# Copies that may run on either engine, norms behind the gathers on VectorE, and unread products in TensorE's pauses

## The chip, the cores and the metric

The kernel runs on one core of a Trainium2 chip. The core has engines that work side by side, each through its own instructions in order: TensorE (PE) multiplies matrices and transposes, VectorE (DVE) and ScalarE (ACT) work elementwise and reduce, GpSimd (POOL) does elementwise work too and issues the indirect DMAs, and SyncE (SP) issues the other DMAs. PE writes into PSUM, which here is eight banks of 128 x 512 f32; DVE and ACT can read them, POOL works on SBUF. Engines wait for each other on semaphores.

The metric is the time of one execution in device microseconds, as the median of several. The program is the same in every execution, and so is its order of instructions.

## The reference

`x` is (8, 128, 128) f32, eight blocks of 128 tokens with 128 features, and `ctx` is (8, 77, 128). There are four layers, each a cross-attention to the context and a second part, both added to `x`:

```python
x = x + L0_xattn(_layernorm(x), ctx)       # 16 heads of 8
x = x + L0_ffn(_layernorm(x))              # soft mixture: 512 slots, exact gelu
x = x + L1_xattn(_layernorm(x), ctx)       # 16 heads of 64, gated
x = x + L1_ffn(_layernorm(x))              # top 3 of 64 experts, capacity 64
x = x + L2_xattn(_layernorm(x), ctx)       # 16 heads of 8, rope, two norms, relu ffn
x = x + L2_ffn(_layernorm(x))              # 6 layers of local attention, 16 heads of 64, window 32
x = x + L3_xattn(_layernorm(x), ctx)       # 8 heads of 64
x = x + L3_ffn(_layernorm(x))              # 2 layers of local attention, 8 heads of 64, window 64
```

The parts that the change touches most are these two. The routed experts of layer 1 (cut):

```python
top_l, top_i = jax.lax.top_k(xf @ gate_w + gate_b, 3)
gates = softmax(top_l)
pos = (cumsum(oh, axis=0) * oh).sum(-1) - 1           # a token's place with its expert
buf = zeros((64, 64, 128)).at[fe, pos].set(xf[tok], mode='drop')
h = gelu(einsum('ecd,edh->ech', buf, w1) + b1)
y = einsum('ech,ehd->ecd', h, w2) + b2
out = zeros_like(xf).at[tok].add(y[fe, pos] * gates)  # three gathered rows a token
```

And one local layer of layer 2 or 3 (cut):

```python
h = shift_token(x)                  # the second half of the features comes from the token before
q, k, v = split(h @ Wqkv)
q, k = rotary(l2norm(q) * qs, l2norm(k) * ks)
x = x + softmax(masked(q k^T * 8)) v @ Wo      # windows: own and the one before
h = layernorm(shift_token(x)) @ W1 + b1
a, g = split(h)
x = x + (a * gelu(g)) @ W2 + b2
```

The cross-attention of layer 2 norms twice inside: `x = norm(query + o)`, a small relu network, `norm(x + ff)`.

## The kernel before

**A planner writes the order.** `Plan` holds steps. A step has a list of engines that may run it with an estimated duration in ns for each (`{"ACT": 591, "DVE": 682}`), the values that it reads and writes, and a function that emits its instructions. `arranged()` plays the steps through when the kernel is built: at each planned time it gives each free engine the earliest ready step it may run, and where a step may run on several engines, the first that is free takes it. A step that opens a value needs a room for it, which for PE's results is one of the eight PSUM banks (`"mm"`). `emit()` then emits the instructions in that order. On the chip each engine holds to its order whatever the real durations are. There are two such plans in the program that runs: "front" (layers 0 and 1 with routing and experts) and "later" (layers 2 and 3). A second, general form of the layers follows under a branch and is not executed for these inputs.

**What the helpers emit.** `Work.copy` brings a PSUM bank to SBUF: on ACT at L749 or, where the caller gave a DVE duration, on DVE at L751. `Work.turn` makes up to four transposes on PE (L762), `Work.mm` one matmul (L769). `Work.normed` and `Work.scaled` make a layer norm: statistics on DVE (L783, L785), then a step on POOL with four small instructions (L776 variance, L790 its power -1/2, L791 and L792 minus mean times that), then the scaling, on ACT (L800) with scale and bias, or on DVE (L802) with mean and scale; with `norms_on_act`, which the later plan sets, on ACT alone.

**Front.** Layer 0's cross-attention (`attend_8`: scores L855, exp L863, sums and products L871, DVE L876 to L878, and the watch on the sums, L881 and L882, on POOL), its soft mixture (up L1215, gelu L1219 with table loads, down L1229), layer 1's cross-attention (`attend_64`), then `Routed`: gate sums and choice on DVE (L1287 to L1348, with L1326 on PE), twelve indirect DMAs on POOL that scatter the rows to their experts (L1363), rows back in (L1421), transposes, and for each expert up (L1461), gelu (L1474) and down (L1482), with the weights streaming in by 256 KB (L1445).

**Later.** For each of eight blocks `one` gathers three rows a token from the expert results (`Routed.gathered`: L1512, an indirect DMA on POOL, and L1517 on DVE, which adds it with its gate), norms, turns, rotates (`Context.rotated`: two DVE products L1549 and an add on POOL, L1553), attends and projects; `layer` does two blocks' norms, relu network and the addition to `x` (L1622 to L1650, with the affine of the norms at L1650 and the addition at L1642 on POOL); `begin` starts local attention for them. In local attention (`Local`) `shifted` turns `y` and copies it with the shift by one token (two copies at L749), `projected` multiplies by Wqkv (L1847), `queries_keys` squares (L1868, ACT), rotates (L1869, L1871 on DVE, L1874 on POOL), scales by the inverse root (L1887, POOL), turns, and copies to `qT` (L749); then scores, exp and products by windows (L1952 to L2019), `divided` (L1981) and the projection (L1933). `gated` is the second part: L2051, gelu on ACT between two table loads (L2058, L2059), L2064, three DVE products L2066, down L2074. The order inside is by halves: four blocks of attention (`some(4)`), then `gated` for four. A half of one layer is called a half layer below.

The two copies in `shifted`, which run on ACT alone:

```python
self.copy(lambda: hs()[0:64], lambda: tp()[0:64], [tp], [hs], 180 + 103 * n)
self.copy(lambda: hs()[64:128, :, 1:P], lambda: tp()[64:128, :, 0 : P - 1], [tp], [hs], 180 + 103 * n)
```

The step in `scaled` that stands on POOL, with `under` being one tensor_scalar for a layer norm:

```python
under(nc, va()[:, 0:n], mv()[:, 0:n, 1])
nc.gpsimd.tensor_tensor(va()[:, n : 2 * n], va()[:, 0:n], c.mhalf[:, 0:n], ALU.pow)
nc.gpsimd.tensor_scalar(nb(), mv()[:, 0:n, 0], -1.0, None, ALU.mult)
nc.gpsimd.tensor_tensor(nb(), nb(), va()[:, n : 2 * n], ALU.mult)
```

## Time and profile before

| what | value |
|---|---|
| median of 3 runs | 1497.15 us (1496.13 to 1500.06) |
| profiled execution | 1488.41 us, of which the span is 1486.4 |
| mean granted TensorE clock in it | 0.977 |
| PE busy | 1389.6 us (93%) |
| DVE, ACT, POOL busy | 918.6, 918.3, 825.9 us |
| routing, first scatter to last | 259.66 to 274.75 us |
| first weights of the experts issued | 281.39 us |
| last result of the experts on its way | 371.55 us |
| gathers, first and last | 374.5 and 422.9 us |
| one half layer of layer 2's local attention, from 675.61 us | 64.98 us |

The profile is of one execution, taken by the hardware; its own time lies 8.74 us under the median of the three runs. The page gives each engine's busy time, then the span in 40 slices of 37.16 us with the busy share in tenths, and the TensorE clock that was granted in each slice. Groups of instructions carry the line of the kernel, the engine and the tiles; behind the bar stand the busy time, the mean duration and the idle time of the engine just before them. Windows cut the span into stretches.

### The profile page before, as it was taken

The numbers are of one execution on the slowest core, as the hardware profiler recorded it, in microseconds if no ns is written. First come the engines' busy times: TensorE is split into PE (matmuls) and PEld (weight loads), VectorE is DVE, ScalarE is ACT, GpSimd is POOL, SyncE is SP. The second block draws the span as 40 slices with busy tenths as digits, with TensorE's granted clock in tenths as the row PEclk, the third lists the DMA queues.
The fourth block names the chain that finished last, engine by engine and source line by source line (L and its number), as shares of the span: only waits on it lengthen the run. The fifth ranks groups of instructions, "written<-read, shape, count | busy, mean of one in ns | idle before, by whom it ended". The sixth has DMA issues, their size and how long they took to land.

```text
span 1486.4 us, 39191 instructions
## 1 busy us (share of the span) xinstructions
PE 1389.6 (93%) x15991; PEld 955.2 (64%) x15991; DVE 918.6 (62%) x1998; ACT 918.3 (62%) x1913; POOL 825.9 (56%) x1282
## 2 busy tenths in 40 slices
PE   8999997798889999999999999999999998889995
PEld 6776675565576666667566666756666666566654
DVE  7542676433459765685958668595866855658563
ACT  4665654343456675766667676666766675667663
POOL 5210235310788975765849586584948662628471
PEclk9999998799799999999999999999999999999997
DMA  9500001597501001000100100010000011000000
GB/s 321 175 1 1 9 5 54 184 337 263 190 13 72 2 2 58 17 2 2 58 17 2 45 31 2 2 58 16 2 2 23 11 65 40 23 2 2 1 9 11
DMA packets 44111, 79.07 MB, mean 53 GB/s; under 512 B 4582, under 2 KB 21542, under 8 KB 42768
## 3 DMA queue, kind: packets, MB, share of 16 engines
q1 hardware_dynamic: 38032, 71.21, 14.0%
q0 software_dynamic: 1536, 3.15, 0.7%
q8 instruction: 128, 2.10, 0.6%
q10 hardware_dynamic: 4352, 2.10, 0.5%
q14 instruction: 63, 0.52, 0.1%
HBM read 67.63 MB, written 8.81 MB: 51 GB/s over the span
## 4 chain that ended last, share of the span: by engine, by line
PE 39%; DVE 17%; POOL 12%; ACT 6%; issue 3%; DMA 2%; POOLq 0%; ACTq 0%; DVEq 0%; SPq 0%
PE mm L1847 7%; PE mm L762 6%; DVE big L1871 4%; DVE big L1869 4%; PE mm L1933 4%; DVE few L1873 4%; POOL big L1874 3%; PE mm L2074 3%; POOL big L1887 3%; PE mm L2019 3%; PE mm L1958 3%; PE mm L2051 3%; PE mm L2064 2%; POOL tiny L790 2%; DMA big<-in_experts_dram 1%
## 5 line engine op out<-in xcount | busy, mean ns | idle before, releaser
L749 ACT COPY big<-mm 128x512 f32<-128x512 f32 (+4 forms) x519 | 278.4, 561 | 220.9 <-PE mm L762 127.3
L1874 POOL TENSOR_TENSOR big<-big,big 128x512 f32<-128x512 f32 x224 | 284.2, 1276 | 225.5 <-DVE big L1871 218.1
L1847 PE MATMUL mm<-wide,big 128*128 128x512 f32 x672 | 317.0, 598 | 8.4 <-ACT big L749 8.4
L762 PE MATMUL mm<-ident,big 128*128 128x128 f32 (+1 forms) x1430 | 204.3, 279 | 26.8 <-DVE big L751 5.3
L1887 POOL TENSOR_TENSOR big<-big,few 128x512 f32<-128x512 f32 x224 | 227.2, 1043 | 1.6
L762 PEld LDWEIGHTS mm<-ident,big 128*128 128x128 f32 (+1 forms) x1430 | 161.4, 142 | 102.9 <-POOL big L1887 35.9
L1869 DVE TENSOR_TENSOR big<-mm,big 128x512 f32<-128x512 f32 x224 | 152.9, 683 | 56.7 <-ACT big L1868 56.2
L1847 PEld LDWEIGHTS mm<-wide,big 128*128 128x128 f32 x672 | 117.3, 191 | 103.6 <-issue 79.4
L1868 ACT ACTIVATE big<-mm 128x512 f32<-128x512 f32 x224 | 133.1, 597 | 77.3 <-PE mm L1847 70.3
L1871 DVE TENSOR_TENSOR big<-mm,big 128x512 f32<-128x512 f32 x224 | 152.7, 682 | 5.3 <-ACT big L1868 5.3
L1873 DVE TENSOR_REDUCE few<-big 128x8 f32<-128x512 f32 x224 | 151.4, 676 | 6.5 <-ACT big L1868 6.5
L1965 ACT ACTIVATE big<-mm 128x512 f32<-128x512 f32 x224 | 118.1, 610 | 28.0 <-PE mm L1958 27.4
L1933 PE MATMUL mm<-narrow,big 128*128 128x128 f32 x896 | 114.0, 279 | 3.7 <-DVE big L1981 3.7
L1933 PEld LDWEIGHTS mm<-narrow,big 128*128 128x128 f32 x896 | 105.6, 192 | 18.0 <-DVE big L1981 12.5
L1975 DVE TENSOR_TENSOR mm<-mm,big 128x512 f32<-128x512 f32 x64 | 44.6, 696 | 117.0 <-ACT big L1974 111.2
L2019 PEld LDWEIGHTS mm<-big,big 128*32 128x32 f32 x3072 | 85.9, 110 | 28.1 <-issue 27.4
L1958 PE MATMUL mm<-big,big 64*64 64x64 f32 (+2 forms) x3584 | 100.4, 238 | 1.1 <-ACT big L749 1.1
L1958 PEld LDWEIGHTS mm<-big,big 64*64 64x64 f32 x3584 | 94.2, 133 | 6.2 <-ACT big L749 2.0
L2019 PE MATMUL mm<-big,big 128*32 128x128 f32 x3072 | 92.8, 273 | 0.0
L1981 DVE SCALAR_TENSOR_TENSOR big<-mm,big 128x512 f32<-128x512 f32 x112 | 73.0, 687 | 5.6 <-PE mm L2019 0.6
L830 POOL TENSOR_TENSOR big<-big,tiny 128x308 f32<-128x308 f32 x40 | 28.5, 717 | 75.0 <-DVE tiny L827 34.2
L1471 DVE TENSOR_TENSOR big<-mm,p_col 128x512 f32<-128x512 f32 x32 | 20.7, 687 | 62.9 <-PE mm L762 53.0
(276 smaller groups left out, 2314.9 us busy)
## 6 DMA issues: line engine op xcount, KB each, us to landing
big<-in_experts_dram SPq DMA_DIRECT2D x128, 256.0 KB
wide<-in_l2a_dram SPq DMA_DIRECT2D x6, 1536.0 KB
narrow<-in_l2b_dram SPq DMA_DIRECT2D x6, 534.0 KB
narrow<-in_l2o_dram SPq DMA_DIRECT2D x6, 512.0 KB
kept<-big SPq DMA_DIRECT2D x16, 154.0 KB
big<-kept SPq DMA_DIRECT2D x16, 154.0 KB
p_w<-in_w_dram SPq DMA_DIRECT2D x1, 2048.0 KB
expert_rows<-big SPq DMA_DIRECT2D x8, 256.0 KB
```

The lines of the kernel that those rows point to most:

```text
L749: nc.scalar.copy(out(), in_())
L762: nc.tensor.transpose(tp()[:, k, :], v(k), c.ident)
L1847: self.plan.add({"PE": 860}, lambda e: nc.tensor.matmul(ps(), lhsT=hs()[:, j, :], rhs=wqkv()[:, o : o + 512], start=True, stop=True), [hs, ...
L1868: yield lambda e: nc.scalar.activation(sq(), heads(), AF.Square)
L1869: yield lambda e: nc.vector.tensor_tensor(t1(), heads(), spread(rot()[:, 2 * kind, :], 8, 1), ALU.mult)
L1871: yield lambda e: nc.vector.tensor_tensor(halves(t2()), halves(heads())[:, :, ::-1, :], sin(), ALU.mult)
L1873: yield lambda e: nc.vector.tensor_reduce(ss()[:, lo : lo + 8], sq(), AX.X, ALU.add)
L1874: yield lambda e: nc.gpsimd.tensor_tensor(t1(), t1(), t2(), ALU.add)
L1887: plan.add({"POOL": 1062}, lambda e, t=t, t1=t1, i=i: nc.gpsimd.tensor_tensor(t(), t1(), spread(r()[:, 8 * i : 8 * i + 8], 64, 2), ALU.mul ...
L1933: nc.tensor.matmul(out(), lhsT=oT()[:, k, :], rhs=wo()[:, 4 * g + k, :], start=(g == 0 and k == 0), stop=(4 * g + k == nch - 1))
L1958: nc.tensor.matmul(sc[s]()[at : at + 64, k, q:end], lhsT=kT()[lo : lo + 64, k, at : at + 64], rhs=qT()[lo : lo + 64, k, q:end], start=Fals ...
L2019: nc.tensor.matmul(avs[half]()[32 * t : 32 * t + 32, k, :], lhsT=vs[t // 2]()[:, at : at + 32], rhs=prs[t]()[:, k, :], start=True, stop=True)
```

## The change

The planner gets a sixth kind of decision. While the planned time lies before a limit (300 us in the plan "front", 60 us in "later", none in the general form), and PE has no step to pick for 400 ns after its last one, it places a matmul whose result nobody reads: `ones` times `ident`, 128 x 128, planned at 220 ns, into the PSUM bank that came free last. More of them follow at once until a step can be picked. In the order that results, 122 of them stand in the part that is executed: 14 ahead of PE's first real matmul, 29 more before some 160 us of the old trace (12 of them before the first L1229), 61 between the matmuls of routing and ahead of the first expert rows, and 18 in the later plan, where the gathers and layer 2's cross-attention are.

The norms behind the gathers (one of a block and two of two blocks for each pair of blocks, 16 in all) are scaled on DVE alone, with mean and scale, and their POOL step has no L791 and L792. The norms of `begin`, `gated` and of the front stay as they were.

The watch, and the add L1553, may run on POOL or DVE. The copies of `shifted` and the copies to `qT` may run on ACT or DVE. The planned duration of a gather goes from 1000 to 1290 ns.

In the order that results, instructions that are executed move like this: on DVE 44 more copies (L751), 17 more scalings (L802), 9 adds (L1553) and 4 pairs of watch instructions; on ACT 44 fewer copies and 17 fewer scalings; on POOL 16 fewer pairs of L791 and L792, 9 fewer adds and 4 fewer watch pairs. SP's list is the same. Of the copies of `shifted`, one pair of layer 2's `begin` and both pairs of layer 3's stand on DVE, the latter ahead of the three products L2066; of the copies to `qT` four and two in turn for each half layer. Where a step changes its engine or its planned time, others move in the order too.

```diff
     DRAIN = 100.0
+    IDLE, WARM = 400.0, 220.0
...
     def __init__(self, tc, rooms):
...
         self.latest, self.previous = {}, None
+        self.warm, self.until = None, 0.0
...
     def fixed(self, tile):
...
         first = 0
+        left, extra, done_on_pe = sum("PE" in s.ns for s in self.steps), 0, True
...
         def open_to(s):
...
                 if pick is None:
+                    if e == "PE" and t < self.until and t >= free[e] + (self.IDLE if done_on_pe else 0.0) and (
+                            rooms["mm"] and left and (coming or any(free[x] > t for x in free if x != e))):
+                        s = Step(first, {e: self.WARM}, self.warm(rooms["mm"][-1]), None, None, 0, None)
+                        s.start, s.engine, free[e], done_on_pe = t, e, t + self.WARM, False
+                        done.append(s)
+                        extra += 1
+                        heapq.heappush(times, free[e])
                     continue
+                if e == "PE":
+                    done_on_pe, left = True, left - 1
                 if e == "PE" and pick.mode not in (None, mode[e]):
...
                 heapq.heappush(times, free[e])
+                if e == "PE" and self.until:
+                    heapq.heappush(times, free[e] + self.IDLE)
                 done.append(s)
...
                         offer(g)
-        assert len(done) == len(self.steps), f"{len(done)} of {len(self.steps)} steps, rooms {rooms}"
+        assert len(done) == len(self.steps) + extra, f"{len(done)} of {len(self.steps)} steps, rooms {rooms}"
         return done
...
     def emit(self):
...
     KINDS = {"tiny": 8, "few": 32, "row": 128, "big": 512, "huge": 1232}
...
-    def __init__(self, c, pool, once, bufs, general):
+    def __init__(self, c, pool, once, bufs, general, warm_until):
         self.c, self.once, self.by_head, self.norms_on_act, self.general = c, once, (0, 1), False, general
         self.plan = Plan(c.tc, {"mm": 8, **bufs})
+        self.plan.until = 0.0 if general else 1e3 * warm_until
+        self.plan.warm = lambda slot: lambda e: c.nc.tensor.matmul(
+            self.buffers["mm"][slot][:, 0:P], lhsT=c.ones, rhs=c.ident, start=True, stop=True)
         self.buffers = {k: [pool.tile([P, n], F32, name=f"{k}{i}") for i in range(bufs[k])]
...
                       reads, writes, "full", opens)
...
-    def normed(self, outs, ins, reads, writes, a=1.0, b=EPS, n=4):
+    def normed(self, outs, ins, reads, writes, a=1.0, b=EPS, n=4, on_dve=False):
...
         self.scaled(outs, ins, reads, writes,
-                    lambda nc, t, v: nc.gpsimd.tensor_scalar(t, v, float(a), float(b), ALU.mult, ALU.add), n)
-
-    def scaled(self, outs, ins, reads, writes, under, n=4):
+                    lambda nc, t, v: nc.gpsimd.tensor_scalar(t, v, float(a), float(b), ALU.mult, ALU.add), n, on_dve)
+
+    def scaled(self, outs, ins, reads, writes, under, n=4, on_dve=False):
         c, nc, plan = self.c, self.c.nc, self.plan
...
             nc.gpsimd.tensor_tensor(va()[:, n : 2 * n], va()[:, 0:n], c.mhalf[:, 0:n], ALU.pow)
-            nc.gpsimd.tensor_scalar(nb(), mv()[:, 0:n, 0], -1.0, None, ALU.mult)
-            nc.gpsimd.tensor_tensor(nb(), nb(), va()[:, n : 2 * n], ALU.mult)
-
-        plan.add({"POOL": 930 + 150 * n}, root, [mv], [va, nb])
+            if not on_dve:
+                nc.gpsimd.tensor_scalar(nb(), mv()[:, 0:n, 0], -1.0, None, ALU.mult)
+                nc.gpsimd.tensor_tensor(nb(), nb(), va()[:, n : 2 * n], ALU.mult)
+
+        plan.add({"POOL": (500 if on_dve else 930) + 150 * n}, root, [mv], [va] if on_dve else [va, nb])
         for k in range(n):
...
                     nc.vector.tensor_scalar(outs(k), ins(k), mv()[:, k, 0:1], scale(k), ALU.subtract, ALU.mult)
...
-            plan.add({"ACT": 490} if self.norms_on_act else {"ACT": 490, "DVE": 450}, scaled,
-                     [*one, mv, va, nb], writes if len(writes) != n else [writes[k]])
+            plan.add({"DVE": 450} if on_dve else {"ACT": 490} if self.norms_on_act else {"ACT": 490, "DVE": 450}, scaled,
+                     [*one, mv, va] if on_dve else [*one, mv, va, nb], writes if len(writes) != n else [writes[k]])
...
     def softmax(self, sc, n, by_head=False):
...
         plan.add({"DVE": 282}, lambda e: nc.vector.tensor_tensor(oT(), av(), rs(), ALU.mult), [av, rs], [oT])
...
         def watch(e):
-            nc.gpsimd.tensor_tensor(cl(), cl(), rs(), ALU.add)
-            nc.gpsimd.tensor_tensor(c.total, c.total, cl(), ALU.add)
-
-        plan.add({"POOL": 650}, watch, [rs, self.total], [cl, self.total])
+            on = nc.gpsimd if e == "POOL" else nc.vector
+            on.tensor_tensor(cl(), cl(), rs(), ALU.add)
+            on.tensor_tensor(c.total, c.total, cl(), ALU.add)
+
+        plan.add({"POOL": 920, "DVE": 560}, watch, [rs, self.total], [cl, self.total])
         return self.projected_8(oT, wo, bias)
...
     def projected_8(self, oT, wo, bias):
...
                     in_offset=bass.IndirectOffsetOnAxis(ap=self.srci[:, b, k : k + 1], axis=0)).ins
...
-            plan.add({"POOL": 1000}, get, [w.landed], [g], tail=2300)
+            plan.add({"POOL": 1290}, get, [w.landed], [g], tail=2300)
             plan.add({"DVE": 382}, lambda e, k=k, g=g: nc.vector.scalar_tensor_tensor(
...
             t.append(tt)
-        plan.add({"POOL": 240 + 2.0 * n * m}, lambda e: nc.gpsimd.tensor_tensor(
+        plan.add({"POOL": 240 + 2.0 * n * m, "DVE": 145 + 1.1 * n * m}, lambda e: (nc.gpsimd if e == "POOL" else nc.vector).tensor_tensor(
             out() if m > 1 else out().unsqueeze(1), t[0](), t[1](), ALU.add), t, [out])
...
     def keys(self, h):
...
         x, (xh, xT, qT, y) = w.xs[b], (w.tile([P, P]) for _ in range(4))
         route.gathered(w, b)
-        w.normed(lambda k: xh(), lambda k: x(), [x], [xh], n=1)
+        w.normed(lambda k: xh(), lambda k: x(), [x], [xh], n=1, on_dve=True)
         tp = w.turn(lambda k: xh(), [xh], n=1)
...
         y1 = w.tile([P, n, P])
-        w.normed(lambda k, y1=y1: y1()[:, k, :], lambda k, y=y: y[k](), y, [y1], n=n)
+        w.normed(lambda k, y1=y1: y1()[:, k, :], lambda k, y=y: y[k](), y, [y1], n=n, on_dve=True)
         affine(w, y1, "L2_xattn_g1", "L2_xattn_b1", n)
...
         y3 = w.tile([P, n, P])
-        w.normed(lambda k, y3=y3: y3()[:, k, :], lambda k, y2=y2: y2()[:, k, :], [y2], [y3], n=n)
+        w.normed(lambda k, y3=y3: y3()[:, k, :], lambda k, y2=y2: y2()[:, k, :], [y2], [y3], n=n, on_dve=True)
         affine(w, y3, "L2_xattn_g2", "L2_xattn_b2", n)
...
         plan.add({"POOL": 150}, lambda e: nc.gpsimd.memset(hs()[64:128, :, 0:1], 0.0), [], [hs])
-        self.copy(lambda: hs()[0:64], lambda: tp()[0:64], [tp], [hs], 180 + 103 * n)
-        self.copy(lambda: hs()[64:128, :, 1:P], lambda: tp()[64:128, :, 0 : P - 1], [tp], [hs], 180 + 103 * n)
+        self.copy(lambda: hs()[0:64], lambda: tp()[0:64], [tp], [hs], 180 + 103 * n, 145 + 134 * n)
+        self.copy(lambda: hs()[64:128, :, 1:P], lambda: tp()[64:128, :, 0 : P - 1], [tp], [hs], 180 + 103 * n, 145 + 134 * n)
         return hs
...
     def projected(self, layer, hs, j, o, opens):
...
             qT = self.tile([P, 4, P])
-            self.copy(qT, tp, [tp], [qT])
+            self.copy(qT, tp, [tp], [qT], 591, 682)
             out.append(qT)
...
 @contextmanager
-def work(c, name, bufs, general=False):
+def work(c, name, bufs, general=False, warm_until=0.0):
     with c.banks("ps_" + name), c.tc.tile_pool(
...
     ) as pool, c.tc.tile_pool(name="s1_" + name, bufs=1, reuse_waits="tile") as once:
-        w = Work(c, pool, once, bufs, general)
+        w = Work(c, pool, once, bufs, general, warm_until)
         yield w
...
 def later_layers(c, a, wl, dram, route, wide, narrow, out):
     room = {"w": (wide, wl.tile([P, 3072], F32, name="wide1")), "wr": (narrow, wl.tile(list(narrow.shape), F32, name="narrow1"))}
-    with work(c, "later", BUFS_C) as w:
+    with work(c, "later", BUFS_C, False, 60.0) as w:
         with_y(w)
...
         with tc.tile_pool(name="w_early", bufs=1, side="right", reuse_waits="tile") as early:
-            with work(c, "front", BUFS_A, general) as w:
+            with work(c, "front", BUFS_A, general, 300.0) as w:
                 route = plan_front(w, early, dram, wide, narrow)
```

## The prediction

> **What bounds the kernel now.** I read the page's busy shares and its 40 slices first, then cut the span into windows at the stage borders, then took groups, waits and timelines inside each window.
>
> ```profile
> PE 1389.6 (93%) x15991; PEld 955.2 (64%) x15991; DVE 918.6 (62%) x1998; ACT 918.3 (62%) x1913; POOL 825.9 (56%) x1282
> ...
> PE   8999997798889999999999999999999998889995
> ...
> PEclk9999998799799999999999999999999999999997
> ```
>
> TensorE (PE) is the bound on average, with 1486.4 - 1389.6 = 96.8 us of idle. The third line has the dips of the granted clock, in slices 7, 8 and 11 (223 to 297 and 372 to 409 us) and the last. The windows tell which stage could give time (columns: window, its length, busy time of PE, weight loads, DVE, ACT, POOL, clock, DMA share, GB/s):
>
> ```profile
> 37.00:148.00 111.00, 110.87 (x906) 81.72 (x897) 45.98 (x115) 71.28 (x160) 16.88 (x28) 1.00 0.17 60
> ...
> 245.00:281.00 36.00, 19.77 (x108) 15.01 (x106) 22.23 (x105) 5.60 (x16) 16.29 (x35) 0.59 0.20 64
> 281.00:371.00 90.00, 80.93 (x800) 53.76 (x800) 29.39 (x48) 42.51 (x79) 7.56 (x11) 0.99 0.87 303
> 373.50:460.00 86.50, 75.98 (x979) 55.87 (x978) 47.59 (x149) 45.23 (x99) 67.99 (x132) 0.88 0.32 107
> 460.00:520.00 60.00, 57.71 (x711) 38.34 (x710) 47.23 (x95) 41.37 (x86) 57.04 (x86) 1.00 0.04 15
> 675.61:740.59 64.98, 64.51 (x799) 43.18 (x799) 44.93 (x81) 43.79 (x85) 44.83 (x65) 1.00 0.10 34
> ```
>
> The first layer's middle (37 to 148) and a half layer of local attention (675 to 741) are PE without pause: nothing done to another engine shortens them, and a matmul added there lengthens them. Routing (245 to 281) is a chain over DVE and GpSimd (POOL) at a low clock. The experts (281 to 371) are a weight stream. From 373.5 to 520, where the expert results are gathered and layer 2's cross-attention starts local attention, POOL is busy 67.99 + 57.04 = 125.0 of 146.5 us, and its gathers have 7.2 us of issue time between them: 132. PE is busy 133.7. Both limits are near each other.
>
> **Norms behind the gathers, adds and watches: POOL gets lighter.** POOL's groups between 371 and 520 us (busy, mean ns | idle before):
>
> ```profile
> L1874 POOL TENSOR_TENSOR big<-big,big 128x512 f32<-128x512 f32 x22 | 27.9, 1276 | 2.7 <-DVE tiny L785 1.9 <-DVE big L1871 0.4
> L1512 POOL DMA_INDIRECT row<-expert_ys,srci x24 | 23.6, 982 | 7.2 <-issue 5.9 <-PE mm L892 0.5 <-DVE tiny L785 0.3
> ...
> L791 POOL TENSOR_SCALAR tiny<-tiny 128x2 f32<-128x2 f32 (+1 forms) x20 | 4.6, 228 | 0.0
> L792 POOL TENSOR_TENSOR tiny<-tiny,tiny 128x2 f32<-128x2 f32 (+1 forms) x20 | 4.0, 200 | 1.7
> ...
> L881 POOL TENSOR_TENSOR row<-row,row 128x128 f32<-128x128 f32 x8 | 3.8, 475 | 0.1
> L882 POOL TENSOR_TENSOR total<-total,row 128x128 f32<-128x128 f32 x8 | 3.6, 455 | 0.6
> L1553 POOL TENSOR_TENSOR row<-row,row 128x128 f32<-128x128 f32 x8 | 3.6, 454 | 0.1
> ```
>
> Of the 20 pairs L791/L792, 16 go (8 norms of one block, 8 of two): 16 x (228 + 200 ns) = 6.9 us. In the new order all eight adds L1553 here go to DVE (3.6 us), and four of the eight watch pairs (4 x 0.93 = 3.7). POOL loses 14.2 us. Its 24 gathers get fewer instructions between them, so the last of them, now at 422.9 us, starts sooner by what stood ahead of it.
>
> DVE gets 24 scalings, of which 17 come from ACT (17 x 0.34, the median of L802 = 5.8 us), 8 adds at 0.29 and 8 watch instructions at 0.29: 10.4 us, on top of 94.8 busy in 146.5. That has cover; without it, it would cost up to 10. It adds no queued wait on POOL. On DVE a scaling waits for POOL's root, with the next gather's accumulation L1517 behind it; L1517 waits 16 us for its DMA anyway.
>
> A rule speaks against this. **The Trainium skill, "SBUF — State Buffer", "Who interferes with whom"**: VectorE and GpSimd share one pair of ports, and a VectorE instruction with two SBUF inputs, or a copy or tensor_scalar in a two-port mode, shuts a GpSimd reader out for its length, or is shut out. If each of the 40 new instructions did so, POOL would get 24 x 0.34 + 16 x 0.29 = 12.8 of its 14.2 us back. The row: L1517, with two SBUF inputs, has a median of 351 ns and a mean of 371, beside a POOL that is 80% busy; one of 24 took 756 ns, as POOL's L881 ran. So the trace prices a meeting at 0.4 us and finds it rare: some 40 x 0.02 = 0.8 us. I take the row.
>
> What is late next is PE: 133.7 of 146.5 us. So at most 12.8 us can be had without a better clock, less waits that stay, such as the first block's chain (2.72 us before 385.03).
>
> **Unread matmuls.** In this stage the clock is the other half (same columns):
>
> ```profile
> 385.00:390.00 5.00, 2.77 (x25) 2.19 (x29) 1.05 (x3) 0.76 (x2) 4.29 (x8) 0.50 0.85 269
> 390.00:395.00 5.00, 4.62 (x65) 3.79 (x61) 1.99 (x7) 2.54 (x5) 3.99 (x9) 0.50 0.85 273
> 395.00:400.00 5.00, 5.00 (x70) 4.31 (x61) 3.18 (x9) 1.39 (x3) 3.67 (x8) 0.50 0.94 345
> ```
>
> 32 matmuls of L855 take 2.00 us here and 1.11 at full clock (24.12 us). PE is busy about 14 us at half clock, so a full clock is worth 7. The rule, **"TensorE: Matmul & The Clock Gate", "What's actually happening"**: half clock after an idle window of about 3.4 us, full after about 3.4 us of sustained work. By it the clock was due by 394, and a few fillers into the pauses of 382 to 389 would save all 7. The rows hold half clock to 400 at 92 and 100% busy, mostly with matmuls on 32 rows or columns. So fillers a few at a time may not lift it: by the row, 0, and the 18 of them in this part (18 x 0.22 = 4.0 us) come out of the gaps. I take half, +3.5.
>
> The stage, then: POOL's 14.2 is capped by PE's 12.8 + 3.5 - 4.0 = 12.3, of which 3 to 4 stay as waits: **8.5 saved, ends 4 and 15**.
>
> In the routing, 61 of the 122 fillers fall between PE's few matmuls, in idle time (36.0 - 19.77 = 16.2 us; 61 x 0.22 = 13.4). They bring full clock to what is on the chain: eight transposes at 278.91 in 2.09 us (1.04 warm) and the turns and sums ahead of the choice. The weight stream behind starts with the first L1461 and keeps its length, so all of it counts: **+1.7, ends -1 and 3**. The twelve scatters (259.66 to 274.75, 1.26 us each on POOL) stay.
>
> At the start, 14 fillers go ahead of PE's first real work at 4.65 us. Cold at about 0.43 each from about 1.5 they would end near 7.5, past that work, but the second context tile comes only at 7.06 and the matmuls to 12 us run cold (two transposes 0.64, warm 0.44): **+0.5, ends -1 and 2**.
>
> Another 29 stand between there and 160 us, twelve of them before L1229, where the chip reached L1229 without a wait. At 0.22 us that is 6.4; PE's pauses in this part (1.5 in 8 to 37, 1.6 in 148 to 160), and the new order ahead of those twelve, where the gelus may be late, take over half: **-2.5, ends -6 and 0**.
>
> **Copies on either engine.** In the steady local layers four or two copies a half layer go from ACT to DVE (0.58 there, 0.69 here), 44.9 busy of 65. PE's waits there sum to 0.47 us a half layer: **0, ends -4 and +4** over ten. Before layer 3's local parts it is different. ACT at 1259 us:
>
> ```profile
> 1261.17 1.28 ACT L2058 ACT_TABLE_LOAD   x1
> 1262.46 1.83 ACT L2058 ACTIVATE big<-mm,p_col 128x512 f32<-128x512 f32 x3
> 1264.31 1.28 ACT L2059 ACT_TABLE_LOAD   x1
> 1265.61 1.17 ACT L749 COPY big<-mm 64x512 f32<-64x512 f32 x2
> ```
>
> The transposes end at 1263.2; both copies queue behind a gelu and its table load, and PE waits 3.56 us. The same happens at 1333.9. In the new order both copies go to DVE, ahead of its trio L2066: 2 x 0.69 after 1263.2 is 1264.7, 2.1 us sooner. Twice: **+4, ends 1 and 8**. The price is a trio later by 1.4 us, covered by PE's projections. Gather costs in the planner move order only: 0.
>
> **Sum.** 8.5 + 1.7 + 0.5 - 2.5 + 0 + 4 = 12.2, from 1488.4 to 1476.2. The profiled execution's 1488.4 lies 8.7 under the median 1497.15 of the runs shown, so the forecast is 1497.15 - 12.2 = **1485**.
>
> **Rivals.** (1) *PE takes POOL's place*: the clock stays at half and the fillers fill nothing, so the stage gives 4 and layer 3 gives 2 to 3: **1491**. For it: the 12 us at half clock though busy. Against it: PE's 3.6 us of waits for L1553 and the gathers' pace. (2) *All of it*: clock full from 383 on, the stage gives 14, layer 3 gives 6, routing 2.5: 22 less, **1475**. (3) *Slower: fillers into a busy PE.* A filler writes the bank freed last, so it stands until that bank's reader (a copy of 0.58 us) is done, and PE works in order. Some 13 groups before 160 us cost 6.4 + 13 x 0.58 = 13.9, some 12 groups after the experts 4.0 + 7 = 11.0, and the relief without clock is 4 + 2.5: **1497 + 24.9 - 6.5 = 1515** at full price, 1503 at half. It decides once fillers add over 12 us of PE time on the path. For it: PE had 0.13 us of pause in 37 to 148. Against it: fillers come only after 0.4 us without planned work. (4) *It does nothing*: front loss and relief cancel, **1497**.
>
> **Numbers.** Chances: forecast 0.55, (1) 0.20, (2) 0.14, (3) 0.06, (4) 0.05. Less than 0.3% (4.5 us) is what this measurement cannot tell from no change; (1) falls inside it with 0.03. Faster 0.86, same 0.08, slower 0.06. The forecast's ends reach 1476 to 1493; with (1) and half of (2), 1473 to 1496.
>
> **What would show it.** Right: the last gather several us sooner; granted clock above 0.9 in 385 to 400; transposes at 279 us in about 1.05; the half-layer period still 65.0; two PE waits of 3.56 us reduced by 2. Wrong: 37 to 148 with more PE time for the same work, a period above 65.3, or PE waiting for DVE's scalings at 390 to 430.

## The result and the profile after

| | before | after |
|---|---|---|
| median | 1496.68 us (6 runs, 1494.41 to 1500.06) | 1488.68 us (6 runs, 1485.44 to 1491.25) |
| profiled execution, its span | 1488.41, 1486.4 us | 1487.03, 1485.2 us |
| mean granted clock in it | 0.977 | 0.988 |

The ratio is 0.9944, with a 95% interval from 0.9926 to 0.9961: 8.0 us, where 12.2 were forecast. The two profiled executions differ by 1.4 us only, since the one of before was unusually quick. Over 54 runs of before the granted clock and the time go together (9.9 us less for each 0.01 of clock, correlation -0.80), with a median of 0.973 where that execution had 0.977. A second profiled execution of the unchanged kernel (1491.66 us, span 1489.7) is therefore used beside the first below. Against it the traces place 4.4 of the 8.0 us, as the table below shows; the rest belongs to executions of which no trace was kept.

The kernel after has other line numbers: 19 more from L1512 on, so L1847 is L1866, L1933 is L1952, L1981 is L2000; L749, L751 and L762 are L766, L768 and L779; L785 (statistics of a norm) is L802, and the scalings L800 and L802 are L818 and L820; L1512 is L1531, L1517 is L1536; the unread product is L728. The page of after, the same three lines:

```profile
PE 1411.6 (95%) x16235; PEld 982.4 (66%) x16235; DVE 960.5 (65%) x2083; ACT 888.2 (60%) x1846; POOL 810.5 (55%) x1231
...
PE   9999998898899999999999999999999999899995
...
PEclk9999999899999999999999999999999999999998
```

PE is busy for 22 us more with the same useful work: the 122 unread products are in it, 0.237 us each at full clock. In these digits the dips of the clock in slices 7 and 11 are gone; one in slice 8 is left. The windows (same columns as before; the last is two half layers of the steady part of layer 2's local attention):

```profile
37.00:148.00 111.00, 110.32 (x882) 82.08 (x874) 47.91 (x110) 68.36 (x155) 16.03 (x27) 1.00 0.20 66
245.00:281.00 36.00, 32.51 (x248) 28.44 (x246) 22.73 (x110) 7.33 (x18) 17.00 (x36) 0.93 0.18 56
281.00:371.00 90.00, 82.05 (x772) 54.96 (x772) 29.60 (x43) 41.85 (x79) 6.67 (x9) 0.95 0.92 312
373.50:460.00 86.50, 78.70 (x1059) 57.97 (x1056) 62.26 (x205) 40.55 (x85) 58.95 (x98) 1.00 0.36 118
460.00:520.00 60.00, 58.60 (x778) 39.93 (x777) 48.54 (x93) 40.23 (x82) 57.52 (x80) 1.00 0.01 2
747.68:879.00 131.32, 129.29 (x1597) 86.70 (x1596) 93.26 (x169) 84.91 (x162) 88.52 (x123) 1.00 0.07 22
```

From 373.5 to 460 POOL went from 67.99 to 58.95 us, DVE from 47.59 to 62.26, and the clock from 0.88 to 1.00. The last row is the bad news: a layer of local attention takes 131.32 us, and it took 130.0 (twice the 64.98 shown before).

To see where time went, each trace is cut at the same instruction: the first scores of layer 1's attention (L946 of before), the first expert matmul (L1461), the first gather (L1512), the 193rd and the 529th projection of local attention (L1847), and the end. Lengths of the stages in us, one profiled execution each, the experiments among them:

| kernel | front | routing | experts | gathers to local | steady local | layer 3 | median |
|---|---|---|---|---|---|---|---|
| before | 149.2 | 131.7 | 93.6 | 331.3 | 454.9 | 325.7 | 1496.7 |
| before, again | 149.5 | 131.2 | 95.4 | 333.0 | 454.9 | 325.6 | 1496.1 |
| **after** | 151.5 | 132.6 | 95.1 | 324.2 | 460.3 | 321.5 | 1488.7 |
| relief_only | 148.8 | 131.9 | 96.7 | 331.0 | 455.1 | 325.0 | 1493.1 |
| hs_only | 149.8 | 131.3 | 95.6 | 332.1 | 454.8 | 323.4 | 1491.3 |
| fill_only | 151.0 | 132.6 | 96.9 | 334.8 | 455.1 | 330.3 | 1499.5 |
| a_nofill | 148.9 | 131.2 | 96.4 | 331.5 | 460.3 | 320.0 | 1489.6 |
| a_qt_act | 150.4 | 132.5 | 96.0 | 328.5 | 455.6 | 323.3 | 1486.2 |
| a_fill_late_qt | 149.7 | 131.1 | 96.7 | 330.2 | 454.8 | 319.7 | 1485.1 |
| a_nofill_qt | 150.5 | 131.4 | 94.8 | 331.1 | 454.9 | 319.5 | 1486.8 |
| a_qt_fill_later | 149.0 | 131.9 | 95.3 | 328.5 | 455.5 | 319.7 | 1485.0 |
| a_fill_dense_qt | 148.9 | 134.6 | 95.6 | 329.2 | 456.0 | 320.3 | 1487.5 |
| a_fill_all_qt | 150.0 | 131.3 | 98.3 | 329.9 | 455.4 | 323.2 | 1486.9 |

Against the second execution of before, the change is +2.0, +1.4, -0.3, -8.8, +5.4 and -4.1: -4.4 in sum. The two executions of before differ by up to 1.8 us in the first four columns and agree to 0.1 in the last two; in the steady one the clock is full in all kernels. A difference of less than 2 us in one of the first four columns is therefore not shown by two rows alone.

### The profile page after: what moved, and what is told of

The parts are those of the page before. It is cut to its first block, busy times and chain, and to the rows that moved or that the text cites. A ratio compares the mean times of both kernels' runs of the same rounds, so it can differ in the third digit from the quotient of the medians.

```text
span 1485.2 us, 39581 instructions
## 1 busy us (share of the span) xinstructions
PE 1411.6 (95%) x16235; PEld 982.4 (66%) x16235; DVE 960.5 (65%) x2083; ACT 888.2 (60%) x1846; POOL 810.5 (55%) x1231
## 4 chain that ended last, share of the span: by engine, by line
PE 46%; DVE 16%; POOL 10%; ACT 5%; issue 3%; DMA 3%; POOLq 0%; DVEq 0%; ACTq 0%; SPq 0%
PE mm L1866 9%; PE mm L779 7%; PE mm L1952 6%; DVE big L1888 3%; DVE big L1890 3%; POOL big L1893 3%; DVE few L1892 3%; POOL big L1906 3%; PE mm L2093 3%; PE mm L2070 3%; PE mm L1977 3%; PE mm L2083 3%; PE mm L2038 2%; PE mm L1480 2%; DVE big L2000 1%
## 5 line engine op out<-in xcount | busy, mean ns | idle before, releaser
L766 ACT COPY big<-mm 128x512 f32<-128x512 f32 (+3 forms) x475 | 253.6, 560 | 223.2 <-PE mm L779 113.4
L1866 PE MATMUL mm<-wide,big 128*128 128x512 f32 x672 | 315.2, 597 | 4.2 <-DVE big L768 3.0
L779 PE MATMUL mm<-ident,big 128*128 128x128 f32 (+1 forms) x1430 | 205.8, 281 | 21.8 <-DVE big L768 7.8
L779 PEld LDWEIGHTS mm<-ident,big 128*128 128x128 f32 (+1 forms) x1430 | 163.0, 144 | 89.5 <-POOL big L1906 29.3
L1866 PEld LDWEIGHTS mm<-wide,big 128*128 128x128 f32 x672 | 117.4, 191 | 101.3 <-issue 84.7
L1892 DVE TENSOR_REDUCE few<-big 128x8 f32<-128x512 f32 x224 | 150.4, 671 | 1.5 <-ACT big L1887 1.5
L1952 PEld LDWEIGHTS mm<-narrow,big 128*128 128x128 f32 x896 | 106.3, 192 | 28.7 <-DVE big L2000 19.9
L1952 PE MATMUL mm<-narrow,big 128*128 128x128 f32 x896 | 115.0, 279 | 10.1 <-DVE big L2000 9.9
L768 DVE COPY big<-mm 128x512 f32<-128x512 f32 (+5 forms) x117 | 75.3, 659 | 63.9 <-PE mm L779 35.7
L2000 DVE SCALAR_TENSOR_TENSOR big<-mm,big 128x512 f32<-128x512 f32 x112 | 73.2, 685 | 5.8 <-PE mm L2038 0.4
```

The source lines that it names most:

```text
L766: nc.scalar.copy(out(), in_())
L779: nc.tensor.transpose(tp()[:, k, :], v(k), c.ident)
L1866: self.plan.add({"PE": 860}, lambda e: nc.tensor.matmul(ps(), lhsT=hs()[:, j, :], rhs=wqkv()[:, o : o + 512], start=True, stop=True), [hs, ...
L1892: yield lambda e: nc.vector.tensor_reduce(ss()[:, lo : lo + 8], sq(), AX.X, ALU.add)
L1952: nc.tensor.matmul(out(), lhsT=oT()[:, k, :], rhs=wo()[:, 4 * g + k, :], start=(g == 0 and k == 0), stop=(4 * g + k == nch - 1))
```

## The experiments

Eleven kernels ran. In those made from the kernel after, what is not named is as in it. Each ratio is against runs of before that were taken beside that kernel (medians 1496.38, 1497.12 and 1497.58 us).

**The kernel before, again.** No edit.

> The kernel before, unchanged, for a second profiled execution and more times. If the first profiled execution of before (1488.4 us, 8.3 under the median of its runs) was an ordinary one whose speed varies with the granted clock, this one lies near 1496 and its longer time is found in stretches at half clock (between 245 and 420 us, or at the start and the end). If executions differ in something else, the clock's dips are the same and the time differs elsewhere.

1496.13 us (14 runs, ratio 1.0, 0.9986 to 1.0015), profiled at 1491.66. The steady stage is the same to 0.1 us; the 3.3 us between the two profiled executions stand in the experts (+1.8) and behind the gathers (+1.7). The dips are not the same: 13.7 and 10.2 us at half clock there in place of 17.1 and 3.4, and one more of 3.4 in the experts. So the first theory holds for these two; for executions without a trace the place of the lost time is not recorded.

**a_nofill: the change without its unread products.**

```diff
-            with work(c, "front", BUFS_A, general, 300.0) as w:
+            with work(c, "front", BUFS_A, general, 0.0) as w:
-    with work(c, "later", BUFS_C, False, 60.0) as w:
+    with work(c, "later", BUFS_C, False, 0.0) as w:
```

> The change without its unread products (both limits 0). My theory: the 29 products before 160 us cost about 3 us of a stretch in which PE has no pause, and those in the routing and behind the experts bring the full clock to work on the path. So layer 1's attention starts 3 us sooner than after the change, the routing lasts 2 us longer than with them, the stage from the first gather to 460 us loses some 3 us of clock: within 3 us of the changed kernel, 1486 to 1492. The rival, that the products carry most of the gain (by the full clock): 1494 or more. The other rival, that they only cost: 1484 or less.

1489.63 us (ratio 0.9957, 0.9940 to 0.9974): within 1 us of the kernel after, though its mean clock is 0.976 (median of its runs) and that of after 0.988. In the table the front is back by 2.6 us and the routing by 1.4; the stage behind the gathers is 7.3 longer. The products bring and cost about the same: the intervals of the two kernels overlap almost whole.

**a_qt_act: the copies to qT on ACT alone.**

```diff
-            self.copy(qT, tp, [tp], [qT], 591, 682)
+            self.copy(qT, tp, [tp], [qT])
```

> The change with the copies to qT on ACT alone, as before. My theory: in the local layers these copies stand ahead of the divisions (L2000) on VectorE and make PE wait for them, 0.65 us in each half layer (period 131.3 us a layer, 130.0 before). Without them the period goes back to 130.0 and the time falls by 5 to 8 us, to about 1482. The rival, that the drift through the local layers comes from the order that the planner finds after a shorter cross-attention, whatever the copies: period stays at 131.3 and the time at 1488.

1486.25 us (ratio 0.9932, 0.9913 to 0.9951): 2.4 less than after, not 5 to 8. The steady stage is back, 455.6 for 460.3, so the mechanism stands and the rival falls. In the profiled execution the rest is lost elsewhere: the clock fell for 10.2 us at 405.7, which did not happen in the profiled execution of after, and the stage behind the gathers took 328.5 for 324.2.

**a_nofill_qt: both edits.**

> The change without unread products and with the copies to qT on ACT alone: GpSimd's relief and the shifted copies are left. My theory: the copies to qT cost 4 us over the local layers (drift of 0.67 us each half layer from 770 to 1160 us), so this is 4 below the change without products (1489.6): 1485 to 1487. The rival, that the copies to qT cost only with the products (2.4 us were seen there): 1488 to 1490.

1486.8 us (ratio 0.9935, 0.9912 to 0.9957), as expected: 2.8 below a_nofill by the medians, whose intervals overlap, and 454.9 for 460.3 in the steady stage, 5.4 less. What PE waits for between 700 and 1160 us (total, times, longest) in after,

```profile
PE mm L1952 <- DVE big L2000: 4.1, 10, 0.6
PE mm L779 <- DVE big L768: 1.8, 4, 0.4
PE mm L1971 <- DVE big L1890: 0.6, 4, 0.2
```

and in a_nofill_qt:

```profile
PE mm L779 <- ACT big L818: 1.6, 7, 0.2
PE mm L1971 <- DVE big L1890: 1.4, 7, 0.2
```

With the copies on VectorE, PE waits for its divisions (L2000) and for the copies themselves; without them both are gone. The layer is 130 us again, with 3.4 us less of VectorE work (columns as above):

```profile
748.03:878.02 129.99, 129.05 (x1597) 86.37 (x1596) 89.87 (x163) 87.57 (x169) 88.36 (x123) 1.00 0.07 22
```

**a_fill_late_qt: no products ahead of 150 us of the plan, qT on ACT.**

```diff
-                    if e == "PE" and t < self.until and ...
+                    if e == "PE" and self.since <= t < self.until and ...
```

Both lines are cut; `since` is 150 us in the plan "front" and 0 in "later".

> The copies to qT on ACT alone, and in the front unread products only from 150 us of the plan on (none before layer 1's attention ends). My theory: the front gets back the 3 us that the changed kernel's front is late by, on top of the 6 of the copies: about 1479. The rival, that the front is late by the order and not by the products: as with the copies alone, 1482.

1485.14 us (ratio 0.9926, 0.9904 to 0.9948). Front and routing take 280.8 us, as in before (280.7 and 280.9) and 2.1 less than in a_qt_act (282.9); the median is 1.1 lower, which these runs cannot tell from nothing, and neither 1479 nor 1482 was met. One place where products cost time is shown by the trace of after. PE between 61 and 69 us:

```profile
61.87 1.05 PE L1207 MATMUL mm<-big,seT 128*128 128x128 f32 x8
62.76 2.84 PE L728 MATMUL mm<-ident,ones 128*128 128x128 f32 x24
65.44 3.74 PE L1248 MATMUL mm<-wide,big 128*128 128x128 f32 x32
```

Twelve products (each is two matmuls here) take 2.8 us, and L1248 starts behind them without a wait. The order of PE's other work ahead of 150 us differs too between these kernels, so products and order are not separated here.

**relief_only: before, with norms, adds and watches as in the change.** Made from a_nofill_qt, with this edit on both copies of `shifted`:

```diff
-[tp], [hs], 180 + 103 * n, 145 + 134 * n)
+[tp], [hs], 180 + 103 * n)
```

> The kernel before with GpSimd's relief alone: the norms behind the gathers scaled on VectorE, the adds L1553 and the watches on either engine, the gather's planned cost; no unread products, no copies moved. My theory: this carries most of the gain, 6 to 8 us, found between the first gather and the local layers (last L871 about 6 us sooner after the first gather than before); time 1489 to 1491. The rival, that the gain is the unread products' clock or the copies before layer 3: 1494 or more.

1493.13 us (ratio 0.9974, 0.9956 to 0.9992): 4.5 less, with an interval from 1.2 to 6.6: between the 6 to 8 expected and the rival. In the profile the stage behind the gathers gives only 0.3 to 2.0. Its clock is low (columns as above):

```profile
373.50:460.00 86.50, 77.29 (x1001) 57.75 (x996) 57.84 (x188) 36.27 (x76) 57.84 (x97) 0.88 0.35 118
```

POOL has its 10 us (57.84 for 67.99), and PE runs at 0.88 as before.

**hs_only: before, with the copies of `shifted` on either engine.** a_nofill_qt with `on_dve=True` taken out of its three callers and watch, add and gather costs as before.

> The kernel before with only the copies of the shifted tiles on either engine. My theory: two PE waits of 3.6 us ahead of layer 3's projections shrink, 2 us each, nothing else moves: 1492 to 1494. The rival, that PE's idle there is taken up by a later wait or by a drop of the clock: 1496, no change.

1491.29 us (ratio 0.9952, 0.9933 to 0.9971): 6.3 less by the runs, 2.2 in layer 3 by the profile, where PE's two waits for the copies fell from 7.1 to 3.0 us in sum, and the clock was at half for 6.8 us more (3.4 at 1253 us, 3.4 near 1460). The other 4 us of the runs' gain are not placed. Together with relief_only's 4.5 it makes 10.8 us, and a_nofill_qt, which is these two edits together, is 10.3 faster than its runs of before: by the medians the gain comes from these two edits.

**fill_only: before, with the unread products.**

> The kernel before with only the unread products (both limits as in the change). My theory: they lose some 3 us in the front and give back 2 to 4 behind the experts, where the clock then stays up: 1494 to 1498 with a mean clock above 0.983. The rival, that the full clock is worth what it says (0.012 of the span is some 9 us of PE time): 1489 or less.

1499.53 us (22 runs, ratio 1.001, 1.0001 to 1.0020): slower by 0.1 to 3.0 us, at a clock of 0.984 (median of its runs). A higher clock alone did not buy time. The windows' row:

```profile
373.50:460.00 86.50, 75.42 (x987) 58.95 (x988) 42.04 (x136) 41.71 (x91) 61.38 (x123) 0.92 0.31 104
```

PE is as busy as before (75.98), but 11.5 us of its time from 371 to 460 are unread products (without the relief the planner places 30 there in place of 18), while POOL is not relieved. This profiled execution is the longest of the 22. Its layer 3, 4.7 us longer than before, holds no product at all, but 13.7 us at half clock; that part is not a cost of the products.

**a_qt_fill_later: products in the first 60 us of the later plan only, qT on ACT.**

> The same with unread products in the first 60 us of the later plan only. My theory: with GpSimd relieved, PE is what the stage behind the gathers waits for, and there the products pay by the clock (3 us or more from the first gather to the second half layer, against the kernel without them), unlike in the kernel with GpSimd at its limit: 1482 to 1484. The rival, that they cost as much as they bring there too: 1486, as without them.

1485.0 us (ratio 0.9932, 0.9909 to 0.9954): between the two, and no different by the runs from a_nofill_qt (0.9935). In the traces the stage behind the gathers takes 328.5 us against 331.1 in a_nofill_qt, and the clock was at half for 10.2 us there in place of 20.5.

**a_fill_dense_qt: twice the products, none ahead of 150 us, qT on ACT.**

```diff
-    IDLE, WARM = 400.0, 220.0
+    IDLE, WARM = 400.0, 120.0
```

> The copies to qT on ACT alone and products from 150 us of the plan, planned at 120 ns in place of 220, so that about twice as many stand in each pause (they take about 240 on the chip). My theory: in the routing the clock fell at 276 us because a window with 1.6 us of pause was only 0.53 busy; with twice the products no window there is, the eight transposes at 282 us take 1.05 us in place of 1.97 and the experts' first matmuls run at full clock: first up 1 to 2 us sooner than with the single products, provided the products do not delay the routing's own matmuls. The rival, that they do: first up later by 1 us or more, and the time above 1486.

1487.5 us (ratio 0.9943, 0.9922 to 0.9963). Both theories have a part. PE in this kernel's trace:

```profile
280.60 1.83 PE L728 MATMUL mm<-ident,ones 128*128 128x128 f32 x14
282.27 1.04 PE L779 MATMUL mm<-ident,big 128*128 128x128 f32 x8
283.54 4.94 PE L1480 MATMUL mm<-big,slots 128*64 128x512 f32 x22 [0.24 <-ACT slots L766]
```

The eight transposes do run at full clock, 1.04 us. But they start no sooner than in after: the products ahead of them and between the gate's matmuls pushed the routing's own work back, and the stage is the longest of the table, 134.6. In a_fill_late_qt, which differs in the planned 220 ns alone, it takes 131.1.

**a_fill_all_qt: products to the end of the later plan, none ahead of 150 us, qT on ACT.**

> A trial at a faster version: the change with the copies to qT on ACT alone, unread products in the front only from 150 us of the plan, and in the later plan to its end, so that layer 3's pauses are filled too. My theory: beside 1485 for the same without the later ones, the two dips of the clock (one window of 6.8 us near 1252, one near 1460) go, 2 to 4 us: 1481 to 1483. The rival, that products in layer 3's pauses delay its own matmuls as much: 1485 or more.

1486.88 us (ratio 0.9929, 0.9909 to 0.9949): the rival's. The clock stays full from 421 us to the last matmul, and layer 3 takes 323.2 us against 319.7 without these products: 29.4 us of unread products from 1189 us on were not all in pauses.

## Why the prediction was right, and where its steps were off

The direction and the range held; of the 12.2 us, 8.0 came by the medians. The stages of the traces account for 4.4: routing is 3.1 us short of its forecast and the steady layers 5.4, and the other columns lie within 0.4 of theirs. So the sum had two steps wrong, and a third, the largest, right in size but not for its reason; the number came closer than its steps did, which is in part luck. By its own steps:

- **The stage behind the gathers, 8.5 forecast:** 8.8 in the profiled execution of after (7.1 against the first of before). The five other kernels with both the relief and the products gave 2.8 to 4.5, so that 8.8 and 8.5 agree is in part luck. POOL in it, from 371 to 520 us (busy, mean ns | idle before):

```profile
L1531 POOL DMA_INDIRECT row<-expert_ys,srci x24 | 23.4, 977 | 7.0 <-issue 6.7 <-DVE tiny L802 0.3
...
L900 POOL TENSOR_TENSOR row<-row,row 128x128 f32<-128x128 f32 x4 | 1.8, 455 | 3.4 <-DVE tiny L802 2.7 <-DVE row L895 0.8
L901 POOL TENSOR_TENSOR total<-total,row 128x128 f32<-128x128 f32 x4 | 1.8, 454 | 0.3
```

  The gathers cover 38.8 us (their starts, 379.2 to 418.0) where they covered 47.5 (374.5 to 422.0). The forecast capped POOL's 14.2 us by PE's idle time, 12.8, and let clock and products nearly cancel (+3.5 - 4.0); by that sum relief alone should have brought as much (rival (1) put the stage at 4 with the clock at half). Against the two executions of before, relief alone brought 0.3 to 2.0 in this stage, products alone made it 1.8 to 3.5 longer, and the six kernels with both are all shorter. What the length goes with is the time at half clock in the stage:

| us at half clock | stage with the relief | stage without it |
|---|---|---|
| 0 | 324.2 (after) | |
| 10.2 | 328.5, 328.5, 329.2 | |
| 13.7 | 329.9, 330.2 | 334.8 (fill_only) |
| 20.5 | 331.0, 331.1 | 331.3, 332.1 |
| 23.9 | 331.5 | 333.0 |

  At the same 20.5 or 23.9 us the relief is worth about 1 us. Most of the 8.8 thus came with the clock, and fill_only shows that a better clock alone does not bring it. Why both are needed is argued from the busy times, not shown: a longer pause of PE also makes the clock fall, each row is one execution, and the medians do not tell the kernels with products from those without, while relief_only's runs gained 4.5 us.

  The port rule, set aside for the row, did bite. From 371 to 520 us the 24 scalings on VectorE have a median of 346 ns in after, as taken, but a mean of 441: seven of them, of 0.48 to 1.06 us, began while POOL ran a product or an addition and ended 0.08 to 0.09 us behind it. With adds and watches the lengths above the medians sum to 3.2 us, where 0.8 was taken. POOL's own instructions kept their lengths, so its relief stood. The clearest meeting is the ninth add that moved (128 x 308, for the keys). In after, POOL started its product 41 ns sooner:

```profile
326.85 2.24 POOL L1580 TENSOR_TENSOR wide<-big,p_cst 128x1232 f32<-128x1232 f32 x1
326.89 2.54 DVE L1572 TENSOR_TENSOR big<-big,big 128x308 f32<-128x308 f32 x1
```

  In a_nofill the add started first:

```profile
320.18 0.48 DVE L1572 TENSOR_TENSOR big<-big,big 128x308 f32<-128x308 f32 x1
320.26 2.49 POOL L1580 TENSOR_TENSOR wide<-big,p_cst 128x1232 f32<-128x1232 f32 x1
```

  In four kernels POOL was first by 41 to 60 ns, and the add took 2.52 to 2.54 us; in five the add was first by 73 to 84 ns, took 0.48, and the product took 2.49 to 2.50 in place of 2.24. Whichever started first held up the other. Here only POOL's next product waited for the add, 0.4 us.
- **The clock there, half of 7 us taken:** in the profiled execution of after it was full, and 390 to 400 us ran without a dip:

```profile
390.00:395.00 5.00, 4.33 (x79) 3.50 (x82) 1.50 (x6) 2.04 (x4) 3.92 (x6) 1.00 0.82 259
395.00:400.00 5.00, 4.20 (x86) 3.26 (x77) 4.22 (x16) 2.04 (x4) 3.42 (x5) 1.00 0.81 255
```

  In the five other kernels with products and relief it fell for 10.2 to 13.7 us in this stage, and for 20.5 to 23.9 in the six without products. Half was a fair price for the time at half clock.
- **Routing, +1.7 forecast:** a step that failed; the stage was 0.9 to 1.4 longer. The forecast took it that 61 products in 16 us of pause hold the clock. PE from 274 us in after:

```profile
274.43 0.49 PE L728 MATMUL mm<-ident,ones 128*128 128x128 f32 x2
276.50 0.42 PE L779 MATMUL mm<-ident,row 128*64 128x128 f32 x1 [1.58 <-DVE row L1415]
276.72 1.20 PE L728 MATMUL mm<-ident,ones 128*128 128x128 f32 x4
277.85 0.79 PE L1424 MATMUL mm<-b,row 64*128 64x128 f32 x2
278.57 2.10 PE L728 MATMUL mm<-ident,ones 128*128 128x128 f32 x8
282.18 1.97 PE L779 MATMUL mm<-ident,big 128*128 128x128 f32 x8 [1.51 <-DMA big<-expert_rows]
```

  The planner's pause was shorter than the chip's. After a real pause of 1.58 us the clock fell, and the transposes that were to gain took 1.97 us instead of 2.09. Kept warm, in a_fill_dense_qt, they gained and the products took it back. The lengthening has another source. a_fill_late_qt and a_fill_all_qt hold the same 61 products, and none ahead of 150 us; their stage takes 131.1 and 131.3 us, as it does without any (131.2 to 131.9). It takes 132.5 or 132.6 in just the three kernels with products ahead of 150 us (after, a_qt_act, fill_only). In these the planner put the rest of the stage in another order, the same in all three, and layer 1's attention, in which no product stands, already takes 97.6 us in place of 97.1. So the 61 products were worth 0, and some 1.2 us came with the order that the earlier ones left behind.
- **Start and front, +0.5 - 2.5:** 2.0 to 2.3 us late at the first scores in after. The three kernels with products there take 150.4 to 151.5 us, the ten without 148.8 to 150.5: 1.5 between the means, and the two ranges meet. Right within that spread; how much is the products and how much the order is not separated.
- **Steady local layers, 0 with ends of -4 and +4 over ten half layers:** the other step that failed, put at nothing and outside its ends. The copies to `qT` cost 5.4 us over the seven half layers of that stage, 0.77 each, and 0.66 each in the window shown (65.66 for 65.0, past the 65.3 that was to show the forecast wrong). The forecast looked at the engines' totals (44.9 busy of 65 us on VectorE). What mattered is that VectorE works in order: the copies stand ahead of divisions that PE needs at once. With them back on ACT the stage takes 454.8 to 456.0 in all six kernels.
- **Layer 3, +4 (1 to 8):** right. PE's waits for the two pairs of copies fell by 4.1 us, the stage by 4.1 in after and by 5.3 to 6.1 in the four kernels without products there in which the clock did not fall before 1440 us. Those waits (total, times, longest) before,

```profile
PE mm L1847 <- ACT big L749: 7.1, 2, 3.6
```

  and after:

```profile
PE mm L1866 <- DVE big L768: 3.0, 2, 1.5
```

  ACT's table load, and VectorE's copies, in after:

```profile
1268.12 1.83 ACT L2077 ACTIVATE big<-mm,p_col 128x512 f32<-128x512 f32 x3
1269.97 1.28 ACT L2078 ACT_TABLE_LOAD   x1
```

```profile
1268.96 1.39 DVE L768 COPY big<-mm 64x512 f32<-64x512 f32 x2 [5.73 <-PE mm L779]
1270.38 2.06 DVE L2085 SCALAR_TENSOR_TENSOR big<-mm,p_col,big 128x512 f32<-128x512 f32 x3
```

  The copies run beside the gelu and end before the load does.

The rival of fillers into a busy PE was right in kind: by themselves they made the kernel 2 us slower (0.1 to 3.0). The price, up to 25 us, was far too high.

A version without the two parts that cost (qT on ACT, products in the later plan only) has a median of 1485.0 us. Its interval against before (0.9909 to 0.9954) overlaps that of the change, so the gain over it is shown for the steady stage (4.8 us in the traces), not for the whole time.

## What to carry to other kernels

An engine that is busy 70% of a stretch still has an order: before moving a copy to it, look at which instruction of the critical engine waits for what will stand behind the copy. Where two limits are near each other, try the edits apart and together: in these traces neither alone shortened the stage by more than 2 us. Matmuls that fill pauses can miss the real pause, as in the routing, and they move the planner's other steps too; a clock that rises in the profile is not yet time. An instruction moved from GpSimd to VectorE can still meet GpSimd there: compare its mean with its median, not the median alone.

## What the hardware showed

In the 13 traces, the granted clock changes in steps of 3.41 us. All 76 falls came after a step in which PE was busy 0.64 or less, and every step below 0.41 was followed by one at half clock; between these, some fell and some did not. So the clock can fall with PE more than half busy. The step that cost the routing its gain, and the next one, in after:

```profile
272.77:276.18 3.41, 1.98 (x12) 1.28 (x11) 1.35 (x5) 0.26 (x1) 2.75 (x7) 1.00 0.17 58
276.18:279.60 3.42, 3.10 (x11) 2.59 (x12) 0.71 (x4) 0.26 (x1) 1.45 (x3) 0.50 0.11 38
```

PE is busy 1.98 of 3.41 us, 0.58, and falls. Rises behind the first 12 us came after steps with 0.87 or more. But 21 steps that were busy throughout did not bring one, 18 of them in stretches of matmuls with 32 rows or columns (L855, L871), where it came a step or more later. That the width is the reason was not tried, and two of the other three were mostly products of 128 x 128 (at 273.6 us in a_fill_late_qt and 273.7 in a_fill_all_qt).
